# Values' bias in the projections of an attention layer: spread over partitions once and added by VectorE

## The chip, the core and the metric

The kernel runs on one core of a Trainium2 chip. The core's engines are TensorE (PE, with its weight loads as PEld), VectorE (DVE), ScalarE (ACT), GpSimd (POOL) and SyncE (SP), which here only issues DMAs. All tensors are fp32. The metric is device time in microseconds (us) for one execution of the program, from runs on the chip. The profile is one execution of its own, and its times are counted from the first instruction.

## The reference, cut to what matters

One block works on 4096 tokens of width 256: half a mixture-of-experts feed-forward layer, an attention layer with 16 heads of 16, and another half feed-forward layer, each added to its input. The change lies in the attention's projections:

```python
def attn(x, qkv_w, qkv_b, proj_w, proj_b):        # x: layernorm of the block's x
    B, S, D, H = (2, 512, 256, 16)
    HD = D // H
    b, s, d = x.shape                             # 1, 4096, 256
    qkv = jnp.einsum('bsd,ed->bse', x, qkv_w) + qkv_b
    qkv = qkv.reshape(b, s, 3, H, HD)
    q = jnp.transpose(qkv[:, :, 0], (0, 2, 1, 3))
    k = jnp.transpose(qkv[:, :, 1], (0, 2, 1, 3))
    v = jnp.transpose(qkv[:, :, 2], (0, 2, 1, 3))
    scores = jnp.einsum('bhqe,bhke->bhqk', q, k) * scale
    out = jnp.einsum('bhqk,bhke->bhqe', softmax(scores), v)
    ...
x = x + 0.5 * ffn(layernorm(x))
x = x + attn(layernorm(x))
x = x + 0.5 * ffn(layernorm(x))
```

The values are `v = x @ Wv + bv`, a 4096x256 matrix and a bias of 256 numbers.

## The kernel before, in words

The program has five stages, one after the other: routing and the first feed-forward layer's shared part, its experts (to about 460 us), `projections` (478 to 627 us), `attention` (635 to some 2800 us), and the second feed-forward layer.

`projections` goes over the tokens in eight chunks of 512 (`for c in range(NQB)`). `manual_schedule(engines=ORDERED)` keeps PE, ACT, DVE and SP to the order of the code, so each engine's queue is the order of the calls below; POOL's order is left to the scheduler. Per chunk c:

1. `turned` (L181, L1040): PE transposes the four normalized token tiles `xn` of the chunk into two PSUM banks, ACT copies them out as `xT` and sums them.
2. `queries_or_keys(c, 0)` (L968 to L980): four products of two records each into each of two banks for the queries. ACT takes every bank out twice, with the bias (`q`) and squared with the bias (`sq`). SP stores the queries with two DMAs into `qd` (L978).
3. `begin(c + 1)`: DVE makes the next chunk's tokens. For each of the chunk's two pairs of token tiles it adds up five rows a token from a loaded tile `y` (`add_up`, L763 to L765: one add of 1024 columns and two of 512), and then SP issues the load of the `y` six token tiles ahead (`fetch`, L759), into one of three buffers. Then DVE normalizes (`normalize`, L145 to L171), and the last thing it makes is `xn`. POOL adds the projection's bias to the tokens (L947) and stores them (L950).
4. `queries_or_keys(c, 1)`: the same for the keys; ACT first clears the chunk's part of `kT` (L957), and SP copies the keys into `kT` with eight DMAs of 16 partitions each (L986). The tiles `q` of queries and keys share three buffers.
5. `norms(c, 0)`: PE sums the queries' squares by head (L995), DVE takes their maximum (L1002).
6. `values(c, xT, 0, QT)`: the values of the four token tiles, two to a PSUM bank (`v_ps`). For each tile PE first multiplies a row of ones with the bias row `bv_sb` (L1008, one contracted row) and then accumulates two products of `xT` with the weights `wv_sb` (L1016). ACT copies each bank into `v` (L1024), which holds 17 columns a head, the last a one.
7. `norms(c, 1)`: the same as 5 for the keys.

Every fp32 product stands in the trace as two records. The eight PSUM banks of the pool `pm` go round under one tag; a chunk takes ten of them. In the last chunk the second half of the values comes after a few small products for a bound on the scores (L1073, L1085); then DVE makes `bound` (L1095), ACT takes its root (L1098, for which it loads a table of functions), POOL takes the maximum over partitions (L1100), and DVE makes `shift` and `flag` (L1102 to L1112), on which a branch and `attention` wait.

SP's queue in a chunk is thus two `qd`, two `y`, eight `kT`, in this order. Their completions go over eight semaphores in turn, and SP waits for the one before it uses it again. The last `y` are loaded at 572.66 us, one alone.

Of the kernel before, what the change touches and what calls it, by code (L numbers as in the profile page):

```python
# [9 lines left out]
F32 = mybir.dt.float32  # L10
# [3 lines left out]
ALU = mybir.AluOpType  # L14
# [4 lines left out]
P = 128  # L19
T = 4096  # L20
D = 256
# [5 lines left out]
NH = 16  # L27
HD = 16
# [33 lines left out]
def kernel(  # L62
# [14 lines left out]
    nc = tc.nc  # L77
# [23 lines left out]
    ones = const.tile([P, P], F32, name="ones")  # L101
# [28 lines left out]
    for i in range(2):  # L130
        for j in range(HG):
            r = j * HP + i * HD
# [7 lines left out]
    def normalize(pool, xt, xn, n, on_act=False):  # L140

        mv = pool.tile([P, n, 2], F32, tag="mv", name="mv")
        for i in range(n):
            st = pool.tile([P, 6], F32, tag="st", name="st")
            nc.vector.bn_stats(st[:], xt[:, i, :])  # L145
            nc.vector.bn_aggr(mv[:, i, :], st[:])
        ve = pool.tile([P, n], F32, tag="ve", name="ve")
        nc.vector.tensor_scalar(ve[:], mv[:, :, 1], EPS, None, ALU.add)

        r = pool.tile([P, n], F32, tag="r", name="r")  # L150
        r2 = pool.tile([P, n], F32, tag="r2", name="r2")
        nc.vector.tensor_scalar(
            r2[:].bitcast(I32), ve[:].bitcast(I32), 1, None, ALU.arith_shift_right
        )
        nc.vector.tensor_scalar(
            r[:].bitcast(I32), r2[:].bitcast(I32), -1.0, float(0x5F3759DF), ALU.mult, ALU.add
        )
        for _ in range(3):
            nc.vector.scalar_tensor_tensor(r2[:], r[:], -0.5, r[:], ALU.mult, ALU.mult)
            nc.vector.tensor_mul(r2[:], r2[:], ve[:])  # L160
            nc.vector.scalar_tensor_tensor(r[:], r2[:], 1.5, r[:], ALU.add, ALU.mult)
        yield
        if on_act:
            nc.vector.scalar_tensor_tensor(r2[:], mv[:, :, 0], -1.0, r[:], ALU.mult, ALU.mult)
        for i in range(n):
            if on_act:
                nc.scalar.activation(
                    xn[i], xt[:, i, :], AF.Identity, bias=r2[:, i : i + 1], scale=r[:, i : i + 1]
                )
            else:  # L170
                nc.vector.tensor_scalar(  # L171
                    xn[i], xt[:, i, :], mv[:, i, 0:1], r[:, i : i + 1], ALU.subtract, ALU.mult
                )
# [581 lines left out]
    def fetch(pool, t, bufs, m=2, rows=KR):  # L755

        y = pool.tile([P, 2, rows, D], F32, tag="y", name="y", bufs=bufs)
        for i in range(0, 2, m):
            nc.sync.dma_start(y[:, i : i + m], by_token[:, t + i : t + i + m, :rows, :])  # L759
        return y  # L760

    def add_up(y, xt, to=None):
        nc.vector.tensor_add(y[:, :, 0:2], y[:, :, 0:2], y[:, :, 2:4])  # L763
        nc.vector.tensor_add(y[:, :, 0], y[:, :, 0], y[:, :, 1])  # L764
        nc.vector.tensor_add(xt, y[:, :, 0], y[:, :, K] if to is None else to)  # L765
# [152 lines left out]
    def projections(layer, side, weights):  # L918

        keep, kT, v, q_first = side  # L920
        wqk_sb, wv_sb, bias_sb, one_row, bv_sb, bproj_sb = weights
        norm = keep.tile([P, 2, NQB], F32, name="norm")
        sums = keep.tile([P, NC, NQB], F32, name="sums")
        with (
# [10 lines left out]
            def begin(c):  # L935

                xt = pool.tile([P, QT, D], F32, tag="x", name="xt")
                for i in range(0, QT, 2):
                    t = c * QT + i
                    add_up(ys_of.pop(t), xt[:, i : i + 2, :])  # L940
                    if t + ahead < NT:
                        ys_of[t + ahead] = fetch(pool, t + ahead, ahead // 2)
                xn = pool.tile([P, QT, D], F32, tag="xn", name="xn")
                rows = [xn[:, i, :] for i in range(QT)]
                for _ in normalize(pool, xt, rows, QT):
                    pass
                nc.gpsimd.tensor_tensor(  # L947
                    xt[:], xt[:], bproj_sb[:].unsqueeze(1).to_broadcast([P, QT, D]), ALU.add
                )
                nc.gpsimd.dma_start(x1_at[:, c * QT : (c + 1) * QT, :], xt[:])  # L950
                return rows
# [52 lines left out]
            def values(c, xT, first, last):  # L1004
                for t in range(first, last, 2):
                    ps = pm.tile([P, 2, D], F32, tag="m", name="v_ps")
                    for a in range(2):
                        nc.tensor.matmul(  # L1008
                            ps[:, a, :],
                            ones[0:1, :],  # L1010
                            bv_sb[:].rearrange("o h r -> o (h r)"),
                            start=True,
                            stop=False,
                        )
                        for cc in range(NC):
                            nc.tensor.matmul(  # L1016
                                ps[:, a, :],
                                xT[:, cc, (t + a) * P : (t + a + 1) * P],
                                wv_sb[:, cc].rearrange("p h r -> p (h r)"),
                                start=False,  # L1020
                                stop=(cc == NC - 1),
                            )
                    t0 = c * QT + t
                    nc.scalar.copy(  # L1024
                        v[:, t0 : t0 + 2, :, 0:HD],
                        ps[:].rearrange("p a (h r) -> p a h r", r=HD),
                    )

            for t in range(0, ahead, 2):
                ys_of[t] = fetch(pool, t, ahead // 2, m=1 if t < QT else 2)  # L1030
            rows = begin(0)
            for c in range(NQB):
                xT = pool.tile([P, NC, QB], F32, tag="xT", name="xT")
                sums_of = iter([sums[:, cc, c : c + 1] for cc in range(NC)])
                for _ in turned(
                    pm,
                    rows,
                    QT,
                    xT,
                    lambda out, ps: nc.scalar.activation(  # L1040
                        out, ps, AF.Identity, accum_out=next(sums_of)
                    ),
                ):
                    pass
                q2 = queries_or_keys(c, 0, xT)
                if c + 1 < NQB:
                    rows = begin(c + 1)
                k2 = queries_or_keys(c, 1, xT)
                norms(c, 0, q2)
                if c < NQB - 1:  # L1050
                    values(c, xT, 0, QT)
                    norms(c, 1, k2)
                    continue

                values(c, xT, 0, QT // 2)
                norms(c, 1, k2)
                read_queries(q_first, 0, 0)
# [12 lines left out]
            ps = pm.tile([P, NG // 2], F32, tag="m", name="kmean_ps")  # L1070
            for h in range(NG // 2):
                for cc in range(NC):
# [4 lines left out]
                        start=(cc == 0),  # L1077
                        stop=(cc == NC - 1),
# [4 lines left out]
            ps = pm.tile([P, 1], F32, tag="m", name="mean_ps")  # L1083
            for h in range(NG // 2):
# [4 lines left out]
                    start=True,  # L1089
                    stop=True,  # L1090
                )
            nc.vector.tensor_copy(most[:, 2:3], ps[:])
            values(NQB - 1, xT, QT // 2, QT)
            bound = small.tile([P, 2], F32, name="bound")
            nc.vector.tensor_scalar(  # L1095
# [408 lines left out]
    with tc.tile_pool(name="keep0", bufs=1) as keep:  # L1504
        layer = Layer(0, keep, 2 * QT, nc.scalar.copy)
        with ExitStack() as later:
            with tc.tile_pool(name="weights", bufs=1) as pool:
                rare, weights = first_front(layer, keep, pool)
                layer.experts(rare, True)
                side = ctx.enter_context(tc.tile_pool(name="side", bufs=1, side="right"))  # L1510
                kv = later.enter_context(
                    tc.tile_pool(name="kv", bufs=1, side="right", reuse_waits="tile")
                )


                kT = kv.tile([P, NG, T], F32, name="kT")
                v = kv.tile([P, NT, NH, HV], F32, name="v")
                q_first = kv.tile([P, QB], F32, name="q0")
                shift, flag = projections(layer, (side, kT, v, q_first), weights)
            large = nc.values_load(flag[0:1, 0:1], min_val=0, max_val=1)  # L1520
            with tc.If(large > 0):
                take_maxima(kT, q_first)
            layer = Layer(1, side, QT, nc.vector.tensor_copy)
            attention(layer, kT, v, shift, side, q_first)
# [116 lines left out]
```

## Time and profile before

| what | value |
|---|---|
| median of 3 runs | 3200.81 us (3198.05 to 3201.06) |
| the profiled execution | 3198.56 us |
| its span, first to last instruction | 3196.8 us |
| PE busy | 3004.9 us (94%) |
| ACT busy | 2331.2 us (73%) |
| DVE busy | 928.8 us (29%) |
| POOL busy | 600.9 us (19%) |
| DMA, mean | 89 GB/s |
| L1008, the bias products: records, each | 64, 374 to 791 ns, median 478 |
| L1016, the values' products: records, each | 128, 379 to 796 ns, median 379 |
| L1024, the values' copies | 16, 587 ns each |

Most of the span is `attention`, and the shares of busy time are its shares. What concerns the change has to be read from the stretch of 478 to 627 us alone. In the lines below, `PE L1016 MATMUL v_ps<-wv_sb,xT 128*128 128x256` is an instruction of line 1016 that writes tile `v_ps` from `wv_sb` and `xT`; x4 counts those that follow each other without a gap. A window's line gives for each engine its busy time and the number of instructions, then the granted share of PE's clock, the busy share of the 16 DMA engines and what they moved. In the timeline an entry in brackets is the idle time before an instruction and what ended it. A line of `SPq` is the issue of a DMA, not its transfer.

### The profile page before, as it was taken

The page shows a single profiled execution, that of the slowest core. Times are in us where ns is not written, and L with a number is a line of the kernel's source. Part 1 is how long each engine was busy: PE and PEld are TensorE (multiplying, and loading weights), DVE is VectorE, ACT ScalarE, POOL GpSimd, SP SyncE. Part 2 cuts the span into 40 slices and gives each one's busy share as a digit, 9 for nine tenths or more (in the row PEclk, how much of TensorE's full clock was granted, in tenths as well). Part 3 has the DMA queues.
Part 4 walks back from the last instruction along what each step waited for, and adds up shares of the span by engine and source line. Part 5 has one row for each costly group of instructions (what it writes and reads, how often), then busy time and mean ns, then how long its engine had stood idle before and what let it go on. Part 6 is the DMA issues. An engine that isn't in the chain of part 4 may idle for free. (4 is left out here: it accounts for less than half of the span.)

```text
span 3196.8 us, 49937 instructions
## 1 busy us (share of the span) xinstructions
PE 3004.9 (94%) x19947; PEld 1033.2 (32%) x19947; DVE 928.8 (29%) x2764; ACT 2331.2 (73%) x3784; POOL 600.9 (19%) x631
## 2 busy tenths in 40 slices
PE   5769969899999999999999999999999999989994
PEld 3436644322222222222222222222222222246662
DVE  6734447300012113102201211220221121064446
ACT  2103325499999999998999999899899999912330
POOL 2757752100000000100000010010000001025770
PEclk8879989899999999999999999999999999989997
DMA  7367768442100000000000000000000000027867
GB/s 255 135 185 265 266 237 224 130 149 78 40 3 30 25 3 16 30 9 3 32 23 3 25 22 11 16 24 16 3 30 25 3 3 29 1 97 263 308 249 275
DMA packets 143424, 282.97 MB, mean 89 GB/s; under 512 B 31552, under 2 KB 84928, under 8 KB 142784
## 3 DMA queue, kind: packets, MB, share of 16 engines
q1 hardware_dynamic: 106624, 180.38, 17.2%
q0 software_dynamic: 30848, 93.89, 8.1%
q10 hardware_dynamic: 5696, 5.28, 0.5%
q8 instruction: 161, 2.64, 0.3%
q14 instruction: 95, 0.78, 0.1%
HBM read 143.02 MB, written 132.26 MB: 86 GB/s over the span
## 5 line engine op out<-in xcount | busy, mean ns | idle before, releaser
L1268 ACT ACTIVATE ex<-banks 128x512 f32<-128x512 f32 (+1 forms) x3227 | 2056.6, 713 | 104.0 <-PE banks L1258 65.3
L1258 PE MATMUL banks<-q,kT 32*128 32x512 f32 x8192 | 1178.4, 641 | 12.9 <-DVE q L1245 11.9
L1288 PE MATMUL banks<-ex,v 128*17 128x512 f32 x8192 | 1078.9, 598 | 0.0
L1258 PEld LDWEIGHTS banks<-q,kT 32*128 32x128 f32 x8192 | 327.8, 183 | 858.4 <-ACT ex L1268 775.6
L363 POOL DMA_INDIRECT xg<-xr,to x128 | 123.7, 967 | 2119.8 <-DVE to L1279 1541.6
L1288 PEld LDWEIGHTS banks<-ex,v 128*17 128x17 f32 x8192 | 136.1, 95 | 777.9 <-issue 776.9
L1309 DVE COPY o<-banks 128x512 f32<-128x512 f32 x32 | 22.1, 692 | 1154.7 <-PE banks L1288 616.6
L746 POOL DMA_INDIRECT ys<-yb,toi x296 | 284.7, 962 | 155.2 <-DVE yb L739 73.2
L707 PE MATMUL h<-xT,w 128*128 128x512 f32 x512 | 232.6, 597 | 0.0
L735 ACT ACTIVATE yb<-o,to 128x256 f32<-128x256 f32 x128 | 53.7, 471 | 144.3 <-PE o L729 129.1
L363 POOL DMA_INDIRECT xg<-xr,sidx x128 | 124.2, 971 | 77.3 <-DVE st L145 38.6
L707 PEld LDWEIGHTS h<-xT,w 128*128 128x128 f32 x512 | 93.4, 193 | 93.2 <-issue 93.2
L729 PE MATMUL o<-w,hT 128*128 128x256 f32 x512 | 121.0, 379 | 0.0
L716 ACT ACTIVATE s<-h 128x512 f32<-128x512 f32 (+1 forms) x104 | 49.4, 475 | 89.2 <-PE h L707 89.1
L678 ACT COPY xT<-xbt_ps 128x512 f32<-128x512 f32 (+1 forms) x104 | 48.2, 463 | 85.9 <-PE xbt_ps L672 84.5
L1312 DVE RECIPROCAL den<-den 128x512 f32<-128x512 f32 x32 | 107.3, 3353 | 1.1
L729 PEld LDWEIGHTS o<-w,hT 128*128 128x128 f32 x512 | 94.2, 190 | 21.4 <-issue 11.5
L718 DVE TENSOR_TENSOR hT<-s,h 128x512 f32<-128x512 f32 (+1 forms) x104 | 55.5, 534 | 150.1 <-PE h L707 143.5
L672 PE MATMUL xbt_ps<-ident,xb 128*128 128x128 f32 x512 | 71.1, 283 | 27.4 <-DMA xb<-xg 26.1
L1279 DVE SCALAR_TENSOR_TENSOR to<-ex,slot 128x2 int32<-128x2 f32 x56 | 9.0, 161 | 299.4 <-ACT ex L1268 299.4
L395 ACT ACTIVATE th<-sh_ps 128x512 f32<-128x512 f32 x22 | 13.1, 598 | 103.8 <-PE sh_ps L386 101.0
L386 PE MATMUL sh_ps<-xT,ws_sb 128*128 128x512 f32 x176 | 81.6, 620 | 4.2 <-PEq L487 4.2
(246 smaller groups left out, 1832.6 us busy)
## 6 DMA issues: line engine op xcount, KB each, us to landing
xb<-xg SPq DMA_DIRECT2D x62, 536.0 KB
w<-in_wexp_dram SPq DMA_DIRECT2D x64, 384.0 KB
xg<-zeros SPq DMA_DIRECT2D x148, 134.0 KB
y<-ys SPq DMA_DIRECT2D x14, 1280.0 KB
y<-ys SPq DMA_DIRECT2D x14, 1024.0 KB
xg<-zero SPq DMA_DIRECT2D x32, 268.0 KB
xbb<-xg SPq DMA_DIRECT2D x40, 134.0 KB
ys<-yb,toi POOLq DMA_INDIRECT x296
```

The source lines that it names most:

```text
L363: ins = nc.gpsimd.indirect_dma_start(out=self.xg[:], out_offset=bass.IndirectOffsetOnAxis(ap=to[:, k : k + 1], axis=0), in_=xr[:, t, :], i ...
L386: nc.tensor.matmul(ps[:], ws13_sb[:, c, h0 : h0 + P], xT[:, c, :], start=(c == 0), stop=(c == NC - 1),)
L672: nc.tensor.transpose(tp[:, i * P : (i + 1) * P], xb[:, i, c * P : (c + 1) * P], ident[:])
L707: nc.tensor.matmul(ps[:, : n * P], w[:, (j * NC + c) * H : (j * NC + c + 1) * H], xT[:, c, : n * P], start=(c == 0), stop=(c == NC - 1),)
L718: nc.vector.tensor_mul(hT[:, : n * P], s1[:, : n * P], h[1][:, : n * P])
L729: nc.tensor.matmul(o[:, i, :], hT[:, (i0 + i) * P : (i0 + i + 1) * P], w2, start=True, stop=True)
L735: nc.scalar.activation(yb[:, i0 + i, :], o[:, i, :], AF.Identity, scale=weight[:, i : i + 1])
L746: ins = nc.gpsimd.indirect_dma_start(out=ys[:], out_offset=bass.IndirectOffsetOnAxis(ap=b["toi"][:, i : i + 1], axis=0), in_=yb[:, i, :], ...
L1258: nc.tensor.matmul(pm.all[:, banks[j], :], kT[rows, g, t * P : (t + 1) * P], q[rows, :], start=True, stop=True,)
L1268: nc.scalar.activation(ex[:, i : i + n, :], pm.all[:, k : k + n, :], AF.Exp, scale=SCALE)
L1288: nc.tensor.matmul(acc[j * HP : j * HP + HV, :], v[:, t, g * HG + j, :], ex[:, j, :], start=(t == 0), stop=(t == NT - 1),)
L1312: nc.vector.reciprocal(den[:], den[:])
```

## The change

The product of ones and bias is made once, ahead of the first chunk, into a bank of its own; ACT copies it to a tile `bv_all` of 128 partitions that all hold the 256 numbers. `values` loses the bias product of each token tile, and its first product starts the accumulation. A bank is taken out by one VectorE `tensor_tensor`, which adds `bv_all` (repeated over the two token tiles) and writes `v`, in place of ScalarE's copy.

```diff
--- before.py
+++ after.py
@@ -1005,29 +1005,35 @@
                 for t in range(first, last, 2):
                     ps = pm.tile([P, 2, D], F32, tag="m", name="v_ps")
                     for a in range(2):
-                        nc.tensor.matmul(
-                            ps[:, a, :],
-                            ones[0:1, :],
-                            bv_sb[:].rearrange("o h r -> o (h r)"),
-                            start=True,
-                            stop=False,
-                        )
                         for cc in range(NC):
                             nc.tensor.matmul(
                                 ps[:, a, :],
                                 xT[:, cc, (t + a) * P : (t + a + 1) * P],
                                 wv_sb[:, cc].rearrange("p h r -> p (h r)"),
-                                start=False,
+                                start=(cc == 0),
                                 stop=(cc == NC - 1),
                             )
                     t0 = c * QT + t
-                    nc.scalar.copy(
+                    nc.vector.tensor_tensor(
                         v[:, t0 : t0 + 2, :, 0:HD],
                         ps[:].rearrange("p a (h r) -> p a h r", r=HD),
+                        bv_all[:].unsqueeze(1).to_broadcast([P, 2, NH, HD]),
+                        ALU.add,
                     )
 
             for t in range(0, ahead, 2):
                 ys_of[t] = fetch(pool, t, ahead // 2, m=1 if t < QT else 2)
+
+            ps = pm.tile([P, D], F32, tag="m", name="bv_ps")
+            nc.tensor.matmul(
+                ps[:],
+                ones[0:1, :],
+                bv_sb[:].rearrange("o h r -> o (h r)"),
+                start=True,
+                stop=True,
+            )
+            bv_all = pool.tile([P, NH, HD], F32, name="bv_all", bufs=1)
+            nc.scalar.copy(bv_all[:].rearrange("p h r -> p (h r)"), ps[:])
             rows = begin(0)
             for c in range(NQB):
                 xT = pool.tile([P, NC, QB], F32, tag="xT", name="xT")
```

## The prediction

> **What bounds the kernel now.** I read the page first. Its chain of waits reaches back only to 3121 us, so it says nothing of this stage: the eight chunks of `projections` run from 478 to 627 us, and I took them window by window. PE transposes chunk c (L181) at 478.3, 496.98, 514.24, 531.50, 548.75, 566.01, 583.27 and 600.53 us: a period of 17.26.
>
> ```profile
> core 0: us, PE busy (x) PEld busy (x) DVE busy (x) ACT busy (x) POOL busy (x), PEclk, DMA share, GB/s
> ...
> 514.24:531.50 17.26, 16.92 (x59) 8.08 (x57) 11.67 (x32) 9.18 (x15) 3.10 (x2) 1.00 0.87 249
> ...
> 548.76:566.02 17.26, 16.92 (x59) 8.08 (x57) 11.67 (x32) 9.18 (x15) 3.11 (x2) 1.00 0.84 252
> ...
> 583.27:600.53 17.26, 16.92 (x59) 8.09 (x57) 11.68 (x32) 9.18 (x15) 3.10 (x2) 1.00 0.49 109
> ```
>
> PE is busy 16.92 of 17.26 us, so the stage is PE's. But DMA stands at 0.84 to 0.87 beside it, until the last loads of `y` are out. Next, what fills PE, in its timeline of chunk 1:
>
> ```profile
> 506.49 0.69 PE L1008 MATMUL v_ps<-bv_sb,ones 1*128 1x256 f32 x2
> 507.12 1.13 PE L1016 MATMUL v_ps<-wv_sb,xT 128*128 128x256 f32 x4
> 508.18 0.69 PE L1008 MATMUL v_ps<-bv_sb,ones 1*128 1x256 f32 x2
> 508.80 1.13 PE L1016 MATMUL v_ps<-wv_sb,xT 128*128 128x256 f32 x4
> ```
>
> Each fp32 matmul is two records. From the start of a bias pair to the start of L1016 is 0.62 us, from there to the next pair 1.06 (4 x 0.265). Third, the evictions, in the groups by line:
>
> ```profile
> L1024 ACT COPY v<-v_ps 128x512 f32<-128x512 f32 x16 | 9.4, 587 | 47.4 <-PE v_ps L1016 47.4
> L739 DVE TENSOR_TENSOR yb<-o,to 128x512 f32<-128x512 f32 x64 | 44.3, 692 | 14.2 <-PE o L729 11.7
> L1002 DVE TENSOR_REDUCE norm<-sq_ps 128x1 f32<-128x512 f32 x16 | 11.0, 688 | 45.6 <-PE sq_ps L995 45.6
> ```
>
> Both engines sit idle until PE has finished. Last, what runs close behind PE: SP's queue, in its timeline, and what DVE makes of a loaded `y`:
>
> ```profile
> 505.32 1.82 SPq L759 DMA_DIRECT2D y<-ys  x2
> 507.24 13.47 SPq L986 DMA_DIRECT2D kT<-q  x8
> ...
> 513.43 0.58 SPq L986 DMA_DIRECT2D kT<-q  x1
> 520.12 0.58 SPq L986 DMA_DIRECT2D kT<-q  x1
> 520.80 1.63 SPq L978 DMA_DIRECT2D qd<-q  x2
> ...
> 572.66 0.45 SPq L759 DMA_DIRECT2D y<-ys  x1
> ...
> 584.81 0.58 SPq L986 DMA_DIRECT2D kT<-q  x1
> ```
>
> ```profile
> 586.66 1.22 DVE L763 TENSOR_TENSOR y<-y 128x1024 f32<-128x1024 f32 x1
> ...
> 593.89 1.38 DVE L171 TENSOR_SCALAR xn<-xt,mv,r 128x256 f32<-128x256 f32 x4
> ```
>
> SP issues 12 DMAs a chunk and waits, before each, for the one eight places earlier. So the seventh `kT` goes when the first `y` of the round has landed (513.4) and the eighth when the second has (520.1); only then come the next `qd` and `y`. SP's waits put 2.3 and 6.1 us to `y<-ys` there. Rounds begin at 503.85, 520.80, 537.56, 554.81 and 571.20: 16.8 us each, hardly under PE's 17.26. **That loop is what is late next.**
>
> **The change part by part.** *Removed on PE:* 32 pairs at 0.62 us, four a chunk: 2.49. Bounds are 0.53 a pair (two records at L1016's spacing) and 0.69 (its busy time). PE's own period becomes 14.77. The last pair, at 620.01, runs at half the granted clock and takes 1.15.
>
> *Moved:* 16 copies of 587 ns leave ACT, 16 adds come to DVE. The nearest row is L739, of the same form (PSUM, a broadcast SBUF operand, SBUF out): 692 ns, which I take. The below bound is 0.59, ACT's copy into the same strided `v`; the upper 2.72, what L764 once took at 480.3 while POOL ran L947, since the first add of a chunk falls into that line's 2.34 us. Cover: DVE is idle 4.8 us before the chunk's second L1002. DVE's work is 11.7 + 1.4 = 13.1 of 14.77 us; at 2.72 for one add it is 15.1, and the cover is gone for 0.3 us of a chunk, 2 us in seven.
>
> *A new wait on DVE:* the adds wait for PE. Queued behind them are the second L1002 and `begin` two chunks on. L1002 waits for squares that PE makes after the values: in chunk 1 ACT's second copy starts at 513.34 and L1002 at 514.38, so an add of 0.69 fits between. So `begin` starts as now, 0.76 us after L181. For the banks, PE comes back to the first `v_ps` bank eight allocations later, in the next chunk's keys, some 8 us after the add: nothing.
>
> *Added:* one pair (0.69) and one 128x256 copy (0.47, as L735) before chunk 0, where PE sits idle 25 us and ACT 26 for the first `xn`: nothing; 1.2 us without that cover. No DMA is added or moved past another; `bv_sb` landed some 290 us earlier.
>
> *The last chunk:* two pairs in its first half, 1.25. Its second half runs from 617.56 to 623.25, 5.69 us. Eight matmuls alone, three before the clock falls and five at 0.53, take 3.5: 2.2 saved (1.4 to 3.4). Then ACT's queue:
>
> ```profile
> 623.27 0.59 ACT L1024 COPY v<-v_ps 128x512 f32<-128x512 f32 x1 [9.18 <-PE v_ps L1016]
> 623.88 1.28 ACT L1098 ACT_TABLE_LOAD   x1
> 625.17 0.20 ACT L1098 ACTIVATE bound<-bound 128x2 f32<-128x2 f32 x1
> ```
>
> From PE's end to the square root is 1.92 us. The table load waits for nothing but the copy before it; with the copy gone it runs early. On DVE the add (0.69) and L1095 (0.23, now behind it) with gaps take 1.0: 0.9 saved (lost 0.4 if the load stays behind L1095).
>
> *The loads.* L181 can start 7.8 us after the chunk's second `y` (586.66 to 593.89, and 0.55 as at 478.3). These landed at 530.4 (chunk 4), 547.3 (5), 563.9 (6) and 584.8 (7). Rounds depend on landings, not on PE, so I leave them there:
>
> - L181 of chunk 4: PE ready at 548.75 - 4 x 2.49 = 538.8, load allows 538.2: no stall.
> - Chunk 5: 553.6 against 555.1: 1.5. Chunk 6: 569.9 against 571.7: 1.8.
> - Chunk 7: PE ready at 586.5. Its load is alone in its round and took 12.1 us from issue; the first of a round takes some 8.1, the second 14. With `kT` now right behind it I take 10.8: landed 583.5, L181 at 591.3 instead of 600.53. Saved there 9.2 (7.9 to 12.0), not the 17.4 of PE alone.
>
> After the last stall of 4.8 us the clock may fall: chunk 0, begun at granted 0.50, took 9.9 us to its L995 and chunk 1 8.5, so 1.4 lost. **Sum:** 9.2 - 1.4 + 1.25 + 2.2 + 0.9 = 12.2 us saved. The profiled execution took 3198.56 us, 1.8 over its span of 3196.8, and 2.25 under the runs' median of 3200.81. Against its time the sum gives 3186.4; I add half the distance to the median: 3187.5.
>
> A round moves 4096 KB (two `y` of 1280, 512 of `x`, two of 256, eight of 64), 4.19 MB. From 505.3 to 520.1 the DMA share is 0.93 at 263 GB/s, so some 14.8 us at full share; and 2.4 us of 0.53 follow in which SP issues. This is why I leave the round at 16.8. By the Trainium skill, DMA: Bandwidth & Descriptors, section Where 436 GB/s comes from, transfers between HBM and SBUF are limited near 358 GB/s: an estimate from that page's figure is 11.7 us a round, the loop would not gate, and the sum would be the first rival's 21.8. No window here sustains that rate over a round.
>
> **The rivals.**
>
> *Full saving.* Rounds shorten once `kT` and `qd` find their data ready. Seven chunks of 2.49 and the last's 4.35 are 21.8: 3177.9. For it: DMA stands at 0.53 between rounds, and chunk 7's `kT` already waits for ACT alone. Against it: in rounds 2 to 4 SP's `qd` waits for ACT 0.4 us at most, and its `kT` up to 6.2 for `y`. The limit in the sentence above would bring it about.
>
> *Rounds a little longer, no change.* The stores of `x` (L950) follow `xn`, so they come 3 to 6 us earlier within SP's rounds and fall among the `y` packets. The DMA view of 516 to 521.5 us holds one whole store (software queue, 0.52 MB, 27.8% of 16 engines): 1.5 us of all engines. With chunk 7's load at 12.1 us the saving is 10.8, less 5 us for each us by which five rounds lengthen; at 1.5 us it is 3.3: 3196.4.
>
> *Slower.* The same collision at full price: each store holds its round up for all of that window, 5.5 us. Five rounds longer by that bring chunk 7's load to 612.3 and L181 to 620.1 instead of 600.5: 19.6 and 1.4 lost, 4.35 saved: 3216. It turns from gain to loss at 2.2 us a round. Against it: the window already reaches 4 us into the second `y`'s time, and its work is 1.5 us.
>
> *It doesn't do what it says.* PE's pace is set by more than the pairs and the four L1016 stretch out; only the last half chunk and the tail (3.1 us) stay: 3196.6. Against it: L968's sixteen run through at 0.44 us each, no gap after any.
>
> **How the numbers follow.** A change under 0.2% (6.4 us) can't be told from none here. Forecast 0.56, full saving 0.22 (both faster: 0.78); longer rounds 0.11 and not as it says 0.04 (same: 0.15); slower 0.07. The forecast's own range, loads between 8.1 us and half a us more a round, is 3183 to 3191. To hold 8 in 10 the range takes in full saving below, with PE's pair at 0.69 (2 us more), and above the longer rounds up to the turning point: 3176 to 3199.
>
> **What would show it.** Right: L181 to L181 at 14.8 us in chunks 1 to 4, then stretched, with waits of DVE's L763 on `y<-ys` of 1 to 6 us; SP's rounds still near 16.8; adds of 0.69; the table load ahead of the last add. Wrong: 14.8 us to the end (full saving), rounds over 19 us (slower), adds over 1.5 us, or PE waiting for DVE to free a bank.

## The result, and the profile after

| what | before | after |
|---|---|---|
| median of 20 runs | 3198.48 us | 3192.15 us |
| ratio, 95% interval | | 0.9981 (0.9975 to 0.9987) |
| span of the profiled execution | 3196.8 us | 3190.3 us |
| chunk 0's L181 to attention's first product | 156.8 us | 150.8 us |
| L181 of chunk 0, chunk 7 | 478.32, 600.53 | 477.15, 597.64 |

The change is faster by about 6 us (0.2%), half of the 12.2 forecast. The time is within the range of 3176 to 3199, but above the forecast's own 3183 to 3191. The two profiled executions show where it arises: attention's first product comes 6.0 us sooner after chunk 0's L181. Of these, 1.7 are gained up to chunk 7's L181, 3.2 from there to the root (L1098, now L1104), and 1.1 behind the root. In these last 1.1 lies a pause of VectorE's before it clears `q`, 1.2 us before the change and 0.1 after it; no run shows that the change shortened it. PE's timeline of the changed kernel (start, length, instruction, idle before it):

```profile
502.98 3.72 PE L1009 MATMUL v_ps<-wv_sb,xT 128*128 128x256 f32 x16
...
507.64 1.09 PE L181 MATMUL tp<-ident,xn 128*128 128x128 f32 x8
...
521.81 1.09 PE L181 MATMUL tp<-ident,xn 128*128 128x128 f32 x8
...
537.59 1.73 PE L181 MATMUL tp<-ident,xn 128*128 128x128 f32 x8 [1.54 <-DVE xn L171]
...
557.37 2.30 PE L181 MATMUL tp<-ident,xn 128*128 128x128 f32 x8 [3.21 <-DVE xn L171]
...
576.26 1.85 PE L181 MATMUL tp<-ident,xn 128*128 128x128 f32 x8 [1.65 <-DVE xn L171]
...
597.64 2.30 PE L181 MATMUL tp<-ident,xn 128*128 128x128 f32 x8 [5.12 <-DVE xn L171]
```

Chunks 1 to 3 follow each other at 14.17 us where it was 17.26. Then PE waits for `xn`, from chunk 4 on, and the distances are 15.8, 19.8, 18.9 and 21.4. The transposes, 1.09 us otherwise, take 1.73 to 2.30 after each wait: at chunk 4 the granted clock is still 1.00 and they follow `xn` tile by tile (their weight loads wait three times 0.18 us for VectorE), at chunks 5 and 7 the clock is 0.50. What DVE waits for, in its waits (total, times, longest) of 478 to 625 us:

```profile
DVE y L763 <- DMA y<-ys: 23.7, 4, 7.7
```

and what SP's queue does, in its waits of 480 to 600 us and its timeline:

```profile
SPq L986 <- DMA y<-ys: 50.6, 11, 6.8
```

```profile
502.45 1.76 SPq L759 DMA_DIRECT2D y<-ys  x2
504.31 14.07 SPq L986 DMA_DIRECT2D kT<-q  x8
...
520.48 1.77 SPq L759 DMA_DIRECT2D y<-ys  x2
522.34 15.43 SPq L986 DMA_DIRECT2D kT<-q  x8
...
539.34 1.83 SPq L759 DMA_DIRECT2D y<-ys  x2
541.25 16.36 SPq L986 DMA_DIRECT2D kT<-q  x8
```

From one first `y` to the next are 18.0, 18.9, 19.8 and 18.9 us, where it was 17.2, 16.5, 17.2 and 16.4: 18.9 on the mean against 16.8. The copies to `kT`, eight issues of 0.6 us, hold SP for 14 to 16 us: they wait for the loads. Over a round the DMA engines are not full, as the windows of two such rounds show (busy time of each engine, granted clock, DMA share, GB/s):

```profile
519.02:537.87 18.85, 16.97 (x62) 8.79 (x60) 13.03 (x35) 8.00 (x13) 3.12 (x2) 1.00 0.80 223
537.87:557.72 19.85, 16.29 (x50) 7.88 (x49) 12.94 (x35) 8.00 (x13) 3.12 (x2) 0.90 0.79 213
```

The share stood at 0.87 in the kernel before. It is a mean of two stretches, here from the first `y` of a round to that of the next, first after the change and then before it:

```profile
520.48:533.48 13.00, 12.66 (x44) 6.14 (x43) 7.70 (x13) 8.00 (x13) 2.37 (x2) 1.00 0.96 281
533.48:539.34 5.86, 4.29 (x20) 2.16 (x18) 5.34 (x23) 0.42 (x1) 0.75 (x1) 1.00 0.44 93
```

```profile
522.53:535.53 13.00, 12.66 (x47) 6.37 (x47) 7.65 (x22) 5.37 (x12) 3.10 (x2) 1.00 0.96 273
535.53:539.07 3.54, 3.54 (x10) 1.54 (x9) 3.37 (x9) 3.09 (x5) 0.00 (x0) 1.00 0.57 175
```

In both kernels the engines are nearly full for 13 us. In the rest of the round SP waits for the second `y` before it can issue the eighth copy, and the engines stand half idle: 3.5 us before, 5.9 after. Last, the adds in the groups by line, and ACT's end of the stage:

```profile
L1017 DVE TENSOR_TENSOR v<-v_ps,bv_all 128x512 f32<-128x512 f32 x16 | 10.6, 683 | 4.6 <-PE v_ps L1009 4.5
```

```profile
609.95 1.28 ACT L1104 ACT_TABLE_LOAD   x1
619.07 0.20 ACT L1104 ACTIVATE bound<-bound 128x2 f32<-128x2 f32 x1 [7.84 <-DVE bound L1101]
```

An add takes 683 ns, and the table load, which stood behind the copy, now starts 8.2 us before the last product ends (618.17).

### The profile page after: what moved, and what is told of

The parts are those of the page before. It is cut to its first block, busy times and chain, and to the rows that moved or that the text cites. A ratio compares the mean times of both kernels' runs of the same rounds, so it can differ in the third digit from the quotient of the medians.

```text
span 3190.3 us, 49813 instructions
## 1 busy us (share of the span) xinstructions
PE 2991.9 (94%) x19885; PEld 1030.1 (32%) x19885; DVE 937.9 (29%) x2780; ACT 2322.6 (73%) x3769; POOL 602.7 (19%) x631
## 3 DMA queue, kind: packets, MB, share of 16 engines
q1 hardware_dynamic: 106624, 180.38, 17.3%
## 5 line engine op out<-in xcount | busy, mean ns | idle before, releaser
L1264 PE MATMUL banks<-q,kT 32*128 32x512 f32 x8192 | 1178.7, 641 | 10.8 <-DVE q L1251 9.8
L729 PEld LDWEIGHTS o<-w,hT 128*128 128x128 f32 x512 | 94.2, 190 | 21.4 <-issue 11.5
L672 PE MATMUL xbt_ps<-ident,xb 128*128 128x128 f32 x512 | 71.0, 283 | 27.3 <-DMA xb<-xg 25.3
```

Source lines behind the costliest of these rows:

```text
L672: nc.tensor.transpose(tp[:, i * P : (i + 1) * P], xb[:, i, c * P : (c + 1) * P], ident[:])
L729: nc.tensor.matmul(o[:, i, :], hT[:, (i0 + i) * P : (i0 + i + 1) * P], w2, start=True, stop=True)
L1264: nc.tensor.matmul(pm.all[:, banks[j], :], kT[rows, g, t * P : (t + 1) * P], q[rows, :], start=True, stop=True,)
```

## The experiments

The kernels ran in three sets of four, each set on one chip with the kernel before beside it. In the first set all kernels took some 5% longer (before: 3370 us), most of it ahead of the projections, so L181 is given from chunk 0's own L181: in the kernel before, chunk 7 comes 122.2 us after it, in the changed kernel 120.5, both from the profiles above, on another chip: the first set has no run of the changed kernel itself. "Rounds" are the distances of the first `y` of SP's rounds 1 to 5. A ratio is a kernel's time over that of the kernel before on the same chip, with its 95% interval.

### First set: the parts, the store, and who issues the loads

**The moved part alone:** the kernel before with its copy on VectorE.

```diff
-                    nc.scalar.copy(
+                    nc.vector.tensor_copy(
                         v[:, t0 : t0 + 2, :, 0:HD],
```

> The bias pairs stay on PE as before the change; the banks are copied out by VectorE instead of ScalarE. Theory (the pairs set the pace, the moved work costs nothing): L181 to L181 stays at 17.26 us, SP's rounds at 16.8, no PE stall; the table load runs early, so about 1 us faster than before. Rival (VectorE's queue gives back part of the gain): L181 to L181 longer than 17.26 or L763 waiting, 2 us or more slower than before.

From chunk 1 on L181 to L181 stayed at 17.26 us with no stall, and the ratio is 1.0002 (0.9986 to 1.0018). That interval is 5 us to each side, so the one microsecond from the table load can't be seen in it; what shows that the move costs PE nothing is the period. SP's rounds were not 16.8: they are 17.3, 17.3, 17.9 and 18.1 us. With the pairs still on PE and the store of `x` in its old place rounds of 18 us thus occur, and at this pace they don't stall PE.

**No store of `x`** in chunks 1 to 6:

```diff
-                nc.gpsimd.dma_start(x1_at[:, c * QT : (c + 1) * QT, :], xt[:])
+                for c1 in {0: [0], NQB - 1: range(1, NQB)}.get(c, ()):
+                    nc.gpsimd.dma_start(x1_at[:, c1 * QT : (c1 + 1) * QT, :], xt[:])
```

> Changed kernel, without the stores of x of chunks 1 to 6 in their chunks: all are written from the last chunk's tokens at its end, so the attention reads wrong residuals. Theory (the store, 3 to 6 us earlier in the round, pushes back the second y): SP's rounds fall from 18.0 to 19.9 us to 16 or less, chunk 7's L181 comes 10 us or more earlier than 597.6. Rival (the rounds are long for another reason, and only the store's own 1.5 us of work goes): rounds of 17 to 18.5 us, chunk 7's L181 some 5 us earlier.

Rounds of 17.3, 17.5, 18.2 and 17.7 us, L181 of chunk 7 at 118.1, which is 2.4 before the changed kernel's on the other chip and not the rival's 5. Theory fell in this form: without any store in chunks 1 to 6 the rounds are still long. (The whole took 3903 us, since other residuals route other tokens later; only the stage is read.)

**The store behind the keys**, on SP:

```diff
                 k2 = queries_or_keys(c, 1, xT)
+                for c1, xt in made:
+                    nc.sync.dma_start(x1_at[:, c1 * QT : (c1 + 1) * QT, :], xt[:])
+                made.clear()
```

> Changed kernel, but the store of x is issued by SP behind the chunk's eight copies to kT, so that it starts when the round's loads have landed. Same bytes. Theory (place of the store): first y lands some 8 us and second some 13.5 us after issue again, rounds near 17.5 us with the store's issue and work in the gap, chunk 7's L181 3 to 7 us earlier than 597.6. Rival (bytes, not place): rounds stay at 18 to 20 us and chunk 7's L181 within 2 us of 597.6.

Rounds of 17.9, 19.6, 20.7 and 18.7, L181 of chunk 7 at 123.5, ratio 0.9999 (0.9985 to 1.0012): the rival's rounds, with chunk 7 3.0 us later than in the changed kernel on the other chip. Behind the copies, where the loads have landed, the store is no cheaper. The edit changes more than the place, though: the store is now also one of SP's DMAs, a thirteenth in its turn.

**The loads issued by POOL:**

```diff
-                        ys_of[t + ahead] = fetch(pool, t + ahead, ahead // 2)
+                        ys_of[t + ahead] = fetch(pool, t + ahead, ahead // 2, eng=nc.gpsimd)
```

> Changed kernel, but the loads of y inside the chunk loop are issued by POOL, so no DMA of SP's waits for their landing. Theory (SP's turn of eight semaphores closes the loop): the loads go out as soon as a buffer is free, no round of 17 to 20 us, L181 to L181 at 14.2 us to the end or nearly, stalls of PE under 4 us in all, 10 to 15 us faster than the changed kernel. Rival (the DMA engines' work of some 15 us a chunk, or POOL's slower issue, sets the pace): L181 to L181 of 15 to 19 us in chunks 4 to 7, gain under 5 us.

No stall in any chunk from 1 on, L181 at 14.17 us to the end and 102.1 us for chunk 7, ratio 0.9919 (0.9887 to 0.9951), more than was expected. The bytes are the same and go through in 14.17 us a chunk, so the transfers did not set rounds of 17 to 20 us. That it was SP's turn is not yet shown by this run alone, since POOL now issues the loads; the third set takes the loop from its other end.

### Second set: against the changed kernel on the same chip

**The changed kernel**, as it is:

> The changed kernel itself, as the measure for the others of this set. The bare repeat: PE stalls from chunk 4 on, rounds of 18 to 20 us, about 6 us faster than before.

Ratio 0.9986 (0.9977 to 0.9995), rounds of 18.3, 19.1, 18.8 and 18.4 us, L181 of chunk 7 at 120.3.

**The store in the middle of the round**, issued by SP between the sixth and seventh copy:

```diff
                     for r in range(0, P, HD):
                         j, k = r // HP * HP, r % HP // HD
+                        if r == 6 * HD:
+                            for c1, xt in made:
+                                nc.sync.dma_start(x1_at[:, c1 * QT : (c1 + 1) * QT, :], xt[:])
+                            made.clear()
```

> Changed kernel, the store of x issued by SP between the sixth and the seventh copy to kT, so that it follows the first y's landing and runs in the second y's tail, where it ran before the change. Same bytes. Theory (place of the store, once more): rounds 1.5 us or more shorter than the changed kernel's of the same set, chunk 7's L181 at least 5 us earlier against chunk 0's. Rival (bytes in flight, wherever they stand): rounds within 0.7 us of the changed kernel's.

Rounds of 17.9, 18.7, 19.1 and 17.8: 18.4 against 18.7 on the mean, L181 of chunk 7 at 118.8, ratio 0.9971 (0.9961 to 0.9982). By the rounds and by chunk 7, 1.5 us earlier instead of 5, theory falls a second time. But the times are not the same: on the mean these runs lie 4.5 us under the changed kernel's on the same chip (2 to 7). Something in this edit is worth that, the place or that SP issues the store, and the profiled execution shows only 1.5 us of it in the stage.

**The removal alone**, with ScalarE's copy and no bias in the values:

```diff
-                        nc.tensor.matmul(
-                            ps[:, a, :],
-                            ones[0:1, :],
-                            bv_sb[:].rearrange("o h r -> o (h r)"),
-                            start=True,
-                            stop=False,
-                        )
...
-                                start=False,
+                                start=(cc == 0),
```

> The pairs are gone, ScalarE copies as before the change, and the values' bias is left out of the result. Theory (loads gate, VectorE's adds are covered): L181 stands where the changed kernel of the same set has it within 2 us at chunk 7, the root comes some 1.3 us later after the last product because the table load is behind the copy again. Rival (adds queued behind the waiting load cost time, or delay the next loads' buffers): chunk 7's L181 4 us or more earlier than the changed kernel's.

Ratio 0.9988 (0.9979 to 0.9997), beside 0.9986 for the changed kernel; rounds of 17.5, 18.9, 18.5 and 18.3, L181 of chunk 7 at 118.0, 2.3 us before the changed kernel's and between the two expectations. The adds cost some 2 us at most there, and nothing that the whole time shows (on the mean 0.7 us between the two, within 2 us of error). ACT's end, with the copy back:

```profile
617.45 0.58 ACT L1017 COPY v<-v_ps 128x512 f32<-128x512 f32 x1 [5.50 <-PE v_ps L1009]
618.05 1.28 ACT L1091 ACT_TABLE_LOAD   x1
619.34 0.20 ACT L1091 ACTIVATE bound<-bound 128x2 f32<-128x2 f32 x1
```

The load is behind the copy again, and the root comes 22.4 us after chunk 7's L181 instead of 21.4. So the moved eviction gains 1.0 us at the end.

**The kernel before, with its loads on POOL** and nothing else:

> The kernel before, with the loads of y of the chunk loop issued by POOL and nothing else. Theory (before, PE alone sets the pace, so free loads are worth nothing): L181 to L181 stays at 17.26 us, same time as before within 2 us. Rival (the loads on POOL bring a gain of their own): faster by more than 4 us.

L181 at 17.26 us from chunk 1 on, ratio 0.9997 (0.9988 to 1.0006). Free loads are worth nothing while PE takes 17.26 us a chunk.

### Third set: the store's share, and the loop from its other end

**The changed kernel, and the changed kernel with no store** in chunks 1 to 6, by the edit of the first set:

> The changed kernel, as the measure for this set: second y of rounds 1 to 4 landing some 16 us after issue, rounds of 18 to 19 us, L181 of chunk 7 some 120.4 us after chunk 0's.

> As the run without stores of x in chunks 1 to 6 (all written at the end from the last chunk's tokens, so the residuals are wrong), now on the same chip as the changed kernel. Theory (the store's bytes, all inside the round since the change, lengthen it): second y lands 1.2 us or more sooner than in the changed kernel of this set, rounds 1.2 to 2.2 us shorter. Rival (the store has no part in it): less than 0.6 us.

The changed kernel had a ratio of 0.9985 (0.9976 to 0.9994), rounds of 18.4, 19.0, 19.7 and 19.3, L181 of chunk 7 at 122.1, and the second `y` of rounds 1 to 4 landing 15.8, 16.1, 16.7 and 16.5 us after issue (the start of the eighth copy). SP's timeline without the store:

```profile
507.28 1.77 SPq L759 DMA_DIRECT2D y<-ys  x2
509.15 15.24 SPq L987 DMA_DIRECT2D kT<-q  x8
...
525.96 1.74 SPq L759 DMA_DIRECT2D y<-ys  x2
...
543.04 1.82 SPq L759 DMA_DIRECT2D y<-ys  x2
...
560.95 1.79 SPq L759 DMA_DIRECT2D y<-ys  x2
...
579.28 0.58 SPq L759 DMA_DIRECT2D y<-ys  x1
```

Rounds of 18.7, 17.1, 17.9 and 18.3, on the mean 18.0 against 19.1, 1.1 us shorter; the second `y` lands 15.2 against 16.3 us after issue, 1.1 sooner. Both are just under the 1.2 that theory asked; L181 of chunk 7 comes at 120.2. (The whole took 3696 us, with other residuals again.) The store takes about 1.1 us of a round. Three executions of the changed kernel itself have means of 18.7, 18.9 and 19.1 and chunk 7 at 120.3 to 122.1, so differences of half a us a round, or of 2 us at chunk 7, are no more than that spread.

**Loads on POOL once more, and the other end of the loop:** the copies to `kT` on POOL, the loads left with SP.

```diff
-                        nc.sync.dma_start(
+                        nc.gpsimd.dma_start(
                             by_group[j : j + HD, :, k, cols], part[r : r + HD, :, :]
                         )
```

> Loads of y issued by POOL in the changed kernel, against the changed kernel on the same chip. Theory: L181 to L181 14.17 us throughout, 102 us from chunk 0 to chunk 7, 17 to 21 us faster than the changed kernel and 22 to 26 us faster than before.

> Changed kernel, the eight copies to kT issued by POOL instead, loads of y and qd left with SP. Theory (SP is held by the copies that wait their turn behind a load, whoever issues the loads): SP is free again, no stalls of PE, L181 to L181 at 14.2 us or nearly, within 6 us of the run with the loads on POOL. Rival (the loads went faster because POOL issued them): rounds and stalls as in the changed kernel.

Loads on POOL: 3172.02 us, ratio 0.9916 (0.9902 to 0.9929), against the changed kernel's 3194.42 in the same set. Copies on POOL: 3175.05, ratio 0.9928 (0.9914 to 0.9942). PE's timeline of the second:

```profile
495.02 1.09 PE L181 MATMUL tp<-ident,xn 128*128 128x128 f32 x8
509.19 1.09 PE L181 MATMUL tp<-ident,xn 128*128 128x128 f32 x8
...
565.86 1.09 PE L181 MATMUL tp<-ident,xn 128*128 128x128 f32 x8
580.03 1.09 PE L181 MATMUL tp<-ident,xn 128*128 128x128 f32 x8
```

and its SP:

```profile
501.60 2.67 SPq L759 DMA_DIRECT2D y<-ys  x2
...
515.75 1.90 SPq L759 DMA_DIRECT2D y<-ys  x2
...
529.92 2.69 SPq L759 DMA_DIRECT2D y<-ys  x2
```

A round of 14.2 us, set by PE, with no stall, though here SP issues the loads. It doesn't matter which of the two leaves SP; they must not share its queue. In both runs SP's waits of 480 to 600 us show no wait for `y`, where the changed kernel has 50.6 us. What is left open is how much is SP's turn of semaphores and how much the transfers' own queue: in both runs the stream that leaves SP also goes over another DMA queue, and no run changed the order within SP's own. The version with the loads on POOL beats both kernels: the change and the loads on POOL save 26 us together, where the one alone saves 4 to 6 and the other alone nothing.

The windows of two chunks with the loads on POOL show how near the next bound is:

```profile
524.93:539.09 14.16, 13.82 (x50) 7.17 (x48) 12.96 (x34) 7.99 (x13) 4.56 (x5) 1.00 0.96 276
539.09:553.26 14.17, 13.83 (x50) 7.18 (x49) 12.97 (x34) 8.00 (x13) 4.56 (x5) 1.00 1.02 294
```

PE is busy 13.8 us of 14.2, DVE 13.0, and the DMA engines are full.

## Why the prediction was right or wrong

*Mechanism.* Right in its main line: PE set the pace, and the loads of `y` by way of SP's queue were next late. The stalls begin at chunk 4 (forecast: 5) and are longest at chunk 7 (5.1 us, forecast 4.8). DVE waits 4.6 to 7.7 us for `y`, where 1 to 6 were forecast. The removal alone has the gain, the move alone changes no period, and the loads alone are worth nothing until the removal is made.

*The step that failed* is "Rounds depend on landings, not on PE, so I leave them there". They rose from 16.8 to 18.9 us. Chunk 7's `y` was put at 583.5 and landed at 589.9: four rounds of 2.1 more, less 2.9 that the first began earlier (1.2 of them because chunk 0 did), and 1.0 from its own landing (11.8 us after issue, not 10.8). L181 of chunk 7 followed it by 7.7 us as computed: 597.6, not 591.3. So what happened is the rival "rounds a little longer", at 2.1 us instead of 1.5. Its cause, the earlier store of `x`, is not shown. Without the store rounds are 1.1 us shorter, but the kernel before has the same stores, and no run took them out there. A place in the round's middle brought 0.3 us of the rounds, one at its end nothing. Nor are the adds the cause: without them, in the removal alone, rounds are 18.3 on the mean against 18.7. And with the pairs kept and the store in its old place, on another chip, rounds of 17.9 and 18.1 us came too, so the 16.8 of one execution need not have been a constant of the loop to begin with. What lengthened the rounds stays open; what is shown is that they gate only while loads and copies share SP's queue. It was not tried to take out `qd`.

*Luck.* Counted from chunk 0's L181, the forecast had 9.2 us saved up to chunk 7's L181 and 2.95 from there to the root. Measured are 1.7 and 3.2, and 1.1 behind the root, where it had nothing. By the longer rounds' own sum (10.8 less 5 us for each us of a round) 2.1 us would have left a saving of 0.3. That 6.3 were measured owes something to terms of neither sum: four rounds lengthened and not five, the first began 1.7 us earlier against chunk 0, and the tail gave 1.1 us whose cause is not shown. The time lies between the forecast (3187.5) and that rival (3196.4), and the range held because it was drawn wide enough to take in both.

*PE's pair* was mis-sized: 2.49 us a chunk, bounds 0.53 to 0.69 a pair, and it is 3.09, or 0.77. The row had L1016 at 0.265 us a record, and without the pairs sixteen run at 0.228 (502.98 to 506.63, where the next line's first product starts). The pairs also cost the products beside them: four pairs at 0.62 and sixteen records at 0.037 more are the 3.09. In the weight loads of 478 to 625 us, idle before each group, before the change:

```profile
L1016 PEld LDWEIGHTS v_ps<-wv_sb,xT 128*128 128x128 f32 x128 | 22.5, 196 | 12.8 <-issue 10.9
L1008 PEld LDWEIGHTS v_ps<-bv_sb,ones 1*128 1x128 f32 x64 | 9.6, 186 | 14.5 <-issue 11.0 <-DVE r L161 2.4 <-DVE norm L1002 1.0
```

and after it:

```profile
L1009 PEld LDWEIGHTS v_ps<-wv_sb,xT 128*128 128x128 f32 x128 | 24.3, 195 | 9.7 <-issue 4.9 <-DVE r L161 1.6
```

Of 27.3 us of such gaps 9.7 are left. A bound from the spacing of the neighbours leaves out what the neighbours lose beside the pairs. While the loads gate, the extra 0.6 us a chunk was worth nothing: PE spent it waiting.

*The full saving* was put at 21.8 us and is 26. Up to chunk 7's L181 it is 20.8 instead of 17.4, which is the pair's size for the most part; the rest lies behind it. That rival came true only in kernels other than the forecast one, as soon as loads and copies were apart.

*DVE's add*: 692 ns forecast, 683 measured; the upper bound of 2.72 beside POOL's L947 did not come. *The last chunk*: from its L181 to the root 24.6 us became 21.4, against 21.7 forecast with the clock's 1.4. *The clock* fell after the shorter stalls too: granted 0.90 and 0.79 of full speed in windows of 537.6 to 554.8 and 554.8 to 571.2. Until chunk 7 PE still came to wait for the loads, so the fall can have cost little there; no run holds the clock to show it. *The added product and copy* and the new wait cost nothing that shows.

*The two figures for the transfers.* By the figure of the Trainium skill, DMA: Bandwidth & Descriptors, section Where 436 GB/s comes from, the prediction estimated rounds of 11.7 us. It took all 4096 KB for transfers between HBM and SBUF, though the 512 KB of copies to `kT` stay within SBUF. Over a chunk the runs with the loads on POOL move 276 and 294 GB/s at a share of 0.96 and 1.02, so 358 is not reached, and the row's 283 at full share was the better figure. But neither figure was what gated: over a round the share was 0.80. The Trainium skill, DMA: Bandwidth & Descriptors, section Issuing engines are not separate DMA queues, says that issuing from several engines saves only the sequencer's time to start a DMA, usually a small thing. Here the gain was 22 us, between 3194.42 and 3172.02, and it was SP's waits that went, not the time to start a DMA.

## What to carry to other kernels

Before taking work from an engine that is busy all the time, look for loops that close just under its period: a queue that waits for its own transfers and comes round in 16.8 us against 17.26 lets only a part of any gain through. A round time read while another engine sets the pace is no constant; treat it as a term with a range of its own. And when a loop of loads gates at a mean DMA share of 0.8, look at the round in parts: if the engines are full in one and half idle in the other, ask which instruction is queued behind a landing, and give that stream another issuer before counting bytes.

## What the runs showed of the hardware that was not expected

A one-row product between full ones cost more than its own records' time: 0.77 us a pair, where a pair is busy for 0.69 and the next product starts 0.62 after it. PE's granted clock fell already behind a stall of 1.54 us, where the prediction counted on it only after 4.8: at chunk 4 it was 1.00 in the transposes (537.59 to 539.33, which take 1.73 us because they wait for the tiles of `xn`) and 0.50 from 540.3 to 543 in the products behind them. And the 16 DMA engines moved 4.17 MB in a chunk's 14.17 us (294 GB/s by 14.17, share 1.02) when POOL issued the loads, but 4.20 and 4.23 MB in rounds of 18.85 and 19.85 us, at shares of 0.80 and 0.79, behind SP's turn.
